# All 3x3 filters made within the first convolution, columns first, and half as many pixels transposed by TensorE ahead of the Gram matrix

## The chip, the cores and the metric

The kernel runs on one core of a Trainium2 chip. The metric is the device time of one execution in microseconds (us). The engines are TensorE (PE in the profile), VectorE (DVE), ScalarE (ACT), GpSimd (POOL) and SyncE (SP). Each works through its own queue in order. DMAs are issued from the queues of SP, POOL and ScalarE.

## The reference

Two bottleneck blocks of a residual network, one after the other, on an input of 64 images with 1024 channels and 14x14 pixels, in float32. One block, shortened:

```python
out = relu(bn(conv1x1(x,   w1) + b1))      # 1024 -> 256 channels
out = relu(bn(conv3x3(out, w2) + b2))      # 256 -> 256, padding 1
out =      bn(conv1x1(out, w3) + b3)       # 256 -> 1024
x   = relu(x + softplus(residual_scale)[0] * out)
```

`bn` takes mean and variance of each channel over all images and pixels (12544 values), so each convolution has to be finished, or its statistics known, before the next can begin.

## The kernel before

All 12544 pixels of the 256 inner channels stay on the chip in `y_all`, 128 channels in two halves. Products of 1x1 convolutions are made by a Strassen-Winograd scheme with seven products instead of eight: class `Seven` names them p1 to p7, and `stream` gives their order over the items, in which p4 and p3 of an item (`last`) come after p1 of the next one:

```python
for now in items:
    yield from now.p1()
    if before is not None:
        yield from before.last()
    yield from now.p6()
    ...
    yield from now.p2(); now.p5(); now.p7()      # each with yield from
```

The stages, in order:

1. **First convolution, layer 0** (about 6 to 322 us). Two images per load of x. The first two loads go through `plain_conv1`, the other thirty in fifteen items of `Conv1` with two loads each. p1, p6, p7 and p4 add up in one bank of the tag `ay` (two buffers); after p1, p6 and p7 ScalarE copies the bank out (`saved`, through `act`, which keeps program order). p2 goes to `ax`, p5 and p3 to `ap` (one buffer each), which VectorE empties with the sum of L346. VectorE also makes four sums of x per item (L354, L355, L356, L373) and the statistics (L349). Beside it, VectorE makes the transformed filters of the 3x3 convolution: `filters`, for six of the eight pieces (layer, input half, output half). The generator is advanced between items: 42 yields over 11 items. It lives in the last 3136 pixels of both halves of `y_all`, which are not yet written. A piece is loaded by SP (L178) into one buffer, its sums are L189, its factors L186, and its six results go to DRAM by POOL (L227).
2. **Second convolution, layer 0** (to about 611 us): a Winograd scheme `conv2`, which reads the filters `us` back from DRAM.
3. **`gram`, layer 0**: the Gram matrix of the normalized pixels, from which the statistics of the third convolution follow without computing it. ScalarE normalizes `y` in pieces of 256, 512, 800 and then seven times 1568 pixels, two halves each (`norm`, L504); `less` takes a centre off: on ScalarE for 1568 pixels in layer 0 (L1199), else on VectorE (L1201). The product needs pixels on the partitions, so they are transposed, 256 at a time (a "pair" of blocks):
   - `by_tensor`: four transposes on TensorE (L904) into PSUM, then a copy by VectorE (L910). The first `FIRST` = 12 pairs and the last one.
   - `by_vector`: SP and POOL first spread 1536 pixels over the partitions by 16 DMAs (`spread`, L896: ten on SP, six on POOL) into one of two `homes`, and VectorE then transposes six pairs out of it (L916). There are `STEPS` = 6 such spreads; spread k + 2 is issued when step k has been transposed.
   Six buffers `zt` lie between VectorE and TensorE. TensorE then multiplies each block by itself (`cp`, `ap`). In layer 0, `gram` also makes the last two pieces of the filters (1, 1, 0) and (1, 1, 1) on VectorE, in twelve portions, in three spare tiles of x.
4. **`conv3_stats`, `residual`**: the statistics of the third convolution, the scale and shift (`affine`), and the first image pair. Two of its eight products are made ahead (`made`), before the statistics; VectorE adds a product to x (L992).
5. **`fused`**, layer 0's third convolution beside layer 1's first one (to about 1315 us), then `conv2`, `gram` (about 1618 to 1695 us), `conv3_stats`, `residual` and `final` for layer 1.

PSUM banks are taken from `Psum`, which hands out tags by a cycle (in layer 1 `cy`, `cx`, two buffers each) unless a tag is named. A scheduler orders the instructions of an engine where they are not pinned by `keep_in_program_order`; TensorE's and `act`'s are pinned.

Of the kernel before, what the change touches and what calls it, by code (L numbers as in the profile page):

```python
# [38 lines left out]
AF = mybir.ActivationFunctionType  # L39
ALU = mybir.AluOpType  # L40

P = 128
# [3 lines left out]
CS = C // P  # L46
MS = M // P
G = 2
T = N // G
# [4 lines left out]
CH = 2  # L54
NZT = 6

FIRST, LAST = 12, 1
RUN = 3 * P
STEP = 4 * RUN
STEPS = (NPX - (FIRST + LAST) * CH * P) // STEP  # L60
# [6 lines left out]
GPX = GI * HW  # L67
RT, NF = 4, 6
# [5 lines left out]
FOUR = 0, 2, 3, 4, 5  # L74
NKS = [4 if i in FOUR else 5 for i in range(NF)]
NK = max(NKS)
D1D2, D0, D3, D1, D2 = range(5)
SUM, DIFF, D0M2, D3M1 = range(4)
ODD, EVEN = range(2)
# [10 lines left out]
def bottlenecks(ctx: ExitStack, tc: tile.TileContext, x, w1s, w2s, w3s, pars, out):  # L90
    nc = tc.nc
# [74 lines left out]

        tc.keep_in_program_order(nc.tensor.matmul(*args, **kw))  # L167

    def filters(eng, b, s, o, spare, pinned=False):

        first, second = spare
        w, n = 3 * P, NK * P
        g = first[:, : 3 * w].rearrange("p (r m) -> p r m", r=3)
        even, quad = first[:, 3 * w : 4 * w], first[:, 4 * w : 5 * w]
        rest, twice = first[:, 5 * w + n :], second[:, 4 * n : 4 * n + w]
        nc.sync.dma_start(out=g, in_=w2s[b][:, s, o])  # L178
        yield

        def run(ins):
            if pinned:
                tc.keep_in_program_order(ins)

        def scaled(to, v, by):
            run(eng.tensor_scalar(to, v, by, None, ALU.mult))  # L186

        def combined(*args):
            run(eng.tensor_tensor(*args))  # L189

        combined(even, g[:, 0], g[:, 2], ALU.add)
        scaled(quad, g[:, 2], 4.0)
        combined(quad, quad, g[:, 0], ALU.add)
        scaled(twice, g[:, 1], 2.0)
        parts = {
            0: (g[:, 0], None, None, 1.0 / 4),
            1: (even, g[:, 1], ALU.add, -1.0 / 6),
            2: (even, g[:, 1], ALU.subtract, -1.0 / 6),
            3: (quad, twice, ALU.add, 1.0 / 24),
            4: (quad, twice, ALU.subtract, 1.0 / 24),  # L200
            5: (g[:, 2], None, None, 1.0),
        }
        for i, (row, more, op, by) in parts.items():

            u = second[:, (i - 1) * n :] if more is not None else first[:, 3 * w :][:, (2 * w if i == 0 else 0) :]
            u = u[:, : NKS[i] * P].rearrange("p (k m) -> p k m", k=NKS[i])
            if more is not None:
                v = rest[:, :w]
                combined(v, row, more, op)
                row = v  # L210
            if i in FOUR:
                r0, r1, r2 = (row[:, k * P : (k + 1) * P] for k in range(3))
                ends = rest[:, w : w + P]
                combined(ends, r0, r2, ALU.add)
                combined(u[:, SUM], ends, r1, ALU.add)
                combined(u[:, DIFF], ends, r1, ALU.subtract)
                scaled(u[:, SUM : DIFF + 1], u[:, SUM : DIFF + 1], 0.5 * by)
                scaled(u[:, D0M2], r0, -by)
                scaled(u[:, D3M1], r2, by)
            else:  # L220
                row = row.rearrange("p (k m) -> p k m", k=3)
                scaled(u[:, D0 : D3 + 1], row[:, 0::2], by)
                scaled(u[:, D1D2], row[:, 1], by)
                combined(
                    u[:, D1 : D2 + 1], u[:, D0 : D3 + 1], u[:, D1D2 : D1D2 + 1].to_broadcast([P, 2, P]), ALU.subtract
                )
            nc.gpsimd.dma_start(out=us[b][i][:, s, o], in_=u)  # L227
            yield

    class Seven:  # L230
# [42 lines left out]
            yield from self.p3()  # L273
            yield from self.p4()

    def stream(items):

        before = None
        for now in items:
            yield from now.p1()  # L280
            if before is not None:
                yield from before.last()
            yield from now.p6()
            if before is not None:
                before.end()
            yield from now.p2()
            yield from now.p5()
            yield from now.p7()
            before = now
        yield from before.last()  # L290
        before.end()

    def act(*args, **kw):

        tc.keep_in_program_order(nc.scalar.activation(*args, **kw))  # L295
# [565 lines left out]
            finished.send(item)  # L861
            queue = queue[1:] + list(itertools.islice(made, 1))

    def conv3(psum, t, o, w3):
        ps = psum.tile()
        for s in range(MS):
            matmul(
                ps.rearrange("p (h l) -> p h l", h=H), w3[:, s, o, :], two(t, s), start=(s == 0), stop=(s == MS - 1)
            )
        return ps  # L870
# [75 lines left out]
                beside[k]()  # L946
        return g0, g1

    def conv3_stats(psum, one, grams, w3, mv):

        g0p, g1p = grams
        g0 = one.tile([P, M + 1], FP, tag="g0", name="g0")
# [188 lines left out]
    with tc.tile_pool(name="first", bufs=1) as one, tc.tile_pool(  # L1141
        name="first_x", bufs=4
    ) as xpool, ExitStack() as scope:
        psum = Psum(scope, ["ps"], ps=4, ay=2)
        w1 = load_w1(one, 0, nc.scalar)
        pair = [load_x(xpool, 0, t, 4 if t == 0 else 2) for t in range(2)]
        for b in range(2):
            p = keep.tile([P, NPAR], FP, tag=f"par{b}", name=f"par{b}")
            nc.scalar.dma_start(out=p, in_=pars[b][:, :NPAR])
            par.append(p)  # L1150
        masks.make_identity(nc, ident)
        w1 = combine_w1(w1, sums_tile(one, 1)[:, 0])

        for t, xt in enumerate(pair):
            plain_conv1(psum, t, xt, w1[0], par[0], stats1)


        spare = [y_all[:, i, NPX - CS * PX :] for i in range(MS)]
        pieces = [(0, 0, 0), (0, 0, 1), (0, 1, 0), (0, 1, 1), (1, 0, 0), (1, 0, 1)]
        work = itertools.chain.from_iterable(filters(nc.vector, *piece, spare) for piece in pieces)  # L1160
        total, free = (1 + NF) * len(pieces), T // 2 - 1 - CS // MS

        def items():
            for i, t in enumerate(range(2, T, 2)):
                xs = [load_x(xpool, 0, t + i) for i in range(2)]
                yield Conv1(psum, one, xs, (t, t + 1), w1, par[0], stats1)
                if i < free:
                    for _ in itertools.islice(work, total * (i + 1) // free - total * i // free):
                        pass

        for _ in stream(items()):
            pass

    for b in range(2):
# [9 lines left out]
        with tc.tile_pool(name=f"last_{b}", bufs=1) as one, tc.tile_pool(  # L1184
# [6 lines left out]
            with ExitStack() as scope:  # L1191
# [3 lines left out]
                    psum = Psum(scope, ["cy", "cx"], cy=2, cx=2, cp=2)  # L1195
                with tc.tile_pool(name=f"gram_{b}", bufs=1) as pool:
                    def less(k, y):
                        if b == 0 and y.shape[-1] == GPX:
                            nc.scalar.activation(y, y, AF.Identity, bias=minus_c[:, k : k + 1])  # L1199
                        else:  # L1200
                            nc.vector.tensor_scalar(y, y, minus_c[:, k : k + 1], None, ALU.add)  # L1201

                    def x_tile(name):
                        return xpool.tile([P, CS * PX], FP, tag="x", name=name)
# [75 lines left out]
```

## Time and profile before

| | |
|---|---|
| median of 3 runs | 2021.53 us (2021.08 to 2023.18) |
| profiled execution: time, span | 2024.42 us, 2022.6 us |
| TensorE matmul (PE) busy | 1955.8 us (97%) |
| VectorE busy | 1603.2 us (79%) |
| ScalarE busy | 927.8 us (46%) |
| GpSimd busy | 599.5 us (30%) |

The profile is that of one execution. A timeline line has start and duration in us, the engine, the line of the kernel, the operation, output<-inputs with their shapes, and how many instructions were merged; the bracket is the time for which the engine stood idle before, and what released it. A line of the list of waits has who waited for whom, us in total, how often, and the longest. A line of the table of windows has the stretch, then the busy us (and instructions) of PE, its weight loads, DVE, ACT and POOL, the clock granted to TensorE, the share of time for which the DMA engines were busy, and GB/s.

### The profile page before, as it was taken

What the parts mean: (1) busy time and instruction counts of PE and PEld (TensorE: products, weight loads), DVE (VectorE), ACT (ScalarE), POOL (GpSimd) and SP (SyncE); (2) the same over time, 40 slices, a digit from 0 to 9 for tenths busy, and PEclk for the clock granted to TensorE, in tenths of its full rate; (3) what the DMA queues carried; (4) which work ended last, traced back from release to release, by engine and by line L of the source; (5) the groups of instructions that cost most, each with busy time, mean ns of one, the idle gap of its engine ahead of it and who ended that gap; (6) DMA issues with size and microseconds to landing.
All of it is one profiled execution on the core that took longest, in us unless ns stands there. A gap on an engine that the chain in (4) does not pass through costs nothing.

```text
span 2022.6 us, 27698 instructions
## 1 busy us (share of the span) xinstructions
PE 1955.8 (97%) x9608; PEld 1647.0 (81%) x9608; DVE 1603.2 (79%) x3070; ACT 927.8 (46%) x1865; POOL 599.5 (30%) x648
## 2 busy tenths in 40 slices
PE   8989999999997999999999999989999899999998
PEld 4545557999996879999999999989999887555554
DVE  6878667999987667677777767689999874899997
ACT  1110113456568135555555555434666450555555
POOL 0101001121212223433343333311212130667665
PEclk9999999999998999999999999999999999999999
DMA  7756443656555814444444444255556455699998
GB/s 278 273 200 243 165 147 121 197 174 201 183 167 167 278 65 187 164 175 177 171 180 163 188 160 184 104 171 183 192 183 193 138 143 207 239 328 334 339 336 302
DMA packets 173661, 404.51 MB, mean 200 GB/s; under 512 B 11601, under 2 KB 141265, under 8 KB 157009
## 3 DMA queue, kind: packets, MB, share of 16 engines
q1 hardware_dynamic: 160608, 328.47, 47.5%
q10 hardware_dynamic: 5328, 50.86, 6.1%
q0 software_dynamic: 7584, 23.40, 3.5%
q8 instruction: 76, 1.25, 0.2%
q14 instruction: 65, 0.52, 0.1%
HBM read 267.95 MB, written 115.87 MB: 190 GB/s over the span
## 4 chain that ended last, share of the span: by engine, by line
PE 51%; DVE 8%; DMA 4%; SPq 1%; issue 1%; ACT 1%; POOL 0%; DVEq 0%; ACTq 0%; POOLq 0%
PE cy L167 13%; PE ay L167 9%; PE cp L167 8%; PE ap L167 5%; PE cx L167 4%; DMA x<-mid 3%; PE even L167 3%; PE odd L167 3%; PE ax L167 3%; PE m L167 2%; PE l L167 2%; DVE x L421 1%; DMA out<-x 1%; SPq L896 1%; DVE x L479 1%
## 5 line engine op out<-in xcount | busy, mean ns | idle before, releaser
L295 ACT ACTIVATE cu<-cy,scale 128x196 f32<-128x196 f32 (+1 forms) x552 | 256.9, 474 | 296.0 <-PE cy L167 288.1
L560 POOL TENSOR_TENSOR diffs<-r 128x448 f32<-128x448 f32 (+1 forms) x80 | 111.9, 1410 | 566.4 <-DVE r L598 290.8
L295 ACT ACTIVATE x<-x,shift 128x392 f32<-128x392 f32 x368 | 211.8, 614 | 68.8 <-POOL x L447 52.6
L421 DVE SCALAR_TENSOR_TENSOR x<-cp,scale,x 128x196 f32<-128x196 f32 (+1 forms) x368 | 177.9, 483 | 82.4 <-PE cp L167 81.3
L167 PE MATMUL cy<-ct,ws 128*128 128x196 f32 (+1 forms) x736 | 221.8, 383 | 2.5 <-ACT cu L295 2.5
L442 POOL TENSOR_TENSOR x<-x,cu 128x196 f32<-128x196 f32 (+1 forms) x184 | 167.9, 912 | 170.6 <-ACT cu L295 170.5
L167 PE MATMUL ay<-at,ws 128*128 128x196 f32 (+1 forms) x752 | 209.3, 381 | 1.0 <-ACT au L295 1.0
L447 POOL TENSOR_TENSOR x<-x,cu 128x392 f32<-128x392 f32 x124 | 125.9, 1015 | 190.7 <-DVE x L421 190.6
L295 ACT ACTIVATE au<-ay 128x196 f32<-128x196 f32 (+1 forms) x141 | 53.7, 381 | 250.3 <-PE ay L167 205.6
L167 PEld LDWEIGHTS ay<-at,ws 128*128 128x128 f32 x752 | 136.6, 190 | 35.4 <-ACT au L295 1.9
L167 PEld LDWEIGHTS cy<-ct,ws 128*128 128x128 f32 x736 | 133.6, 190 | 36.9 <-ACT cu L295 3.8
L468 POOL TENSOR_TENSOR x<-x,cu 128x392 f32<-128x392 f32 x120 | 125.1, 1042 | 82.1 <-DVE x L421 76.9
L167 PE MATMUL m<-sums,ua 128*128 128x224 f32 (+1 forms) x752 | 145.5, 336 | 0.0
L167 PEld LDWEIGHTS m<-sums,ua 128*128 128x128 f32 x752 | 131.4, 189 | 0.2
L167 PE MATMUL cp<-zt 128*128 128x257 f32 x392 | 121.4, 391 | 10.4 <-DVE zt L916 10.4
L421 DVE SCALAR_TENSOR_TENSOR x<-cx,scale,x 128x196 f32<-128x196 f32 (+1 forms) x184 | 89.1, 484 | 50.1 <-PE cx L167 49.8
L167 PE MATMUL cy<-y,w 128*128 128x196 f32 (+1 forms) x412 | 128.0, 397 | 0.0
L167 PE MATMUL cx<-y,w 128*128 128x196 f32 (+1 forms) x404 | 125.6, 396 | 0.7 <-DVE x L992 0.7
L167 PE MATMUL even<-v,ub 128*128 128x224 f32 (+1 forms) x640 | 123.8, 335 | 0.8 <-ACT even L654 0.8
L167 PE MATMUL odd<-v,ub 128*128 128x224 f32 (+1 forms) x640 | 123.8, 335 | 0.2
L167 PE MATMUL l<-diffs,ub 128*128 128x224 f32 (+1 forms) x640 | 122.0, 333 | 0.0
L167 PE MATMUL ap<-x,ws 128*128 128x196 f32 (+1 forms) x376 | 107.5, 390 | 10.2 <-DVE y L346 10.2
(214 smaller groups left out, 4360.1 us busy)
## 6 DMA issues: line engine op xcount, KB each, us to landing
x<-in_x SPq DMA_DIRECT2D x62, 1568.0 KB, 6.8
ub<-u SPq DMA_DIRECT2D x80, 768.0 KB, 4.8
x<-mid SPq DMA_DIRECT2D x32, 1568.0 KB, 10.0
mid<-x ACTq DMA_DIRECT2D x31, 1568.0 KB, 5.2
out<-x SPq DMA_DIRECT2D x124, 392.0 KB, 6.8
ua<-u SPq DMA_DIRECT2D x96, 256.0 KB, 3.1
ub<-u SPq DMA_DIRECT2D x16, 1024.0 KB, 6.3
home<-y SPq DMA_DIRECT2D x90, 96.0 KB, 3.8
```

Of the source, the lines that this page charges most:

```text
L167: tc.keep_in_program_order(nc.tensor.matmul(*args, **kw))
L295: tc.keep_in_program_order(nc.scalar.activation(*args, **kw))
L421: nc.vector.scalar_tensor_tensor(v, bank, self.scale[:, o : o + 1], v, ALU.mult, ALU.add)
L442: nc.gpsimd.tensor_add(self.part(1, 1), self.part(1, 1), u3)
L447: nc.gpsimd.tensor_add(v, v, self.u12)
L468: nc.gpsimd.tensor_add(v, v, self.u12[:, i * self.n : (i + 1) * self.n])
L479: nc.vector.tensor_scalar(v, v, self.shift[:, o : o + 1], 0.0, ALU.add, ALU.max)
L560: nc.gpsimd.tensor_sub(diffs, r[:, :, :, :WH], r[:, :, :, WH:])
L896: queue.dma_start(out=x[32 * i : 32 * i + 32, :, j], in_=y_all[32 * j : 32 * j + 32, :, a : a + RUN])
```

## The change

`filters` becomes one generator for all eight pieces. It adds up the columns first, for all three rows together, and then the rows; sums and scalar_tensor_tensor run on VectorE, factors on ScalarE through `act`; a piece is loaded while the one before is worked on, into the other of two buffers. It has eleven steps per piece. `stream` calls `beside` six times per item, which advances the generator by one or two steps, so that all eight pieces are made within the first convolution. The filters leave `gram`, with their spare tiles. `FIRST` goes from 12 to 6, so `STEPS` from 6 to 7. `less` runs on VectorE throughout. The banks of `made` and of `conv3_stats` are named instead of taken from the cycle.

```diff
-FIRST, LAST = 12, 1
+FIRST, LAST = 6, 1
...
+FSTEPS = 11
...
-    def filters(eng, b, s, o, spare, pinned=False):
+    def filters(pieces, spare):
         first, second = spare
...
+        n, w = 4 * P, 3 * P
+        def view(v, a, k):
+            return v[:, a * P : (a + k) * P].rearrange("p (k m) -> p k m", m=P)
+        rows = first[:, : 3 * n].rearrange("p (r k m) -> p r k m", r=3, m=P)
+        c2, c4, c3 = (view(first, 12 + 4 * i, 4) for i in range(3))
+        c1 = view(second, 18, 5)
+        loads = []
+        def load(piece):
+            b, s, o = piece
+            g = second[:, len(loads) % 2 * 3 * w :][:, : 3 * w]
+            nc.sync.dma_start(out=g.rearrange("p (r m) -> p r m", r=3), in_=w2s[b][:, s, o])
+            loads.append(g.rearrange("p (r k m) -> p r k m", r=3, m=P))
         def run(ins):
-            if pinned:
-                tc.keep_in_program_order(ins)
+            tc.keep_in_program_order(ins)
...
+        def sums(to, a, b, op):
+            run(nc.vector.tensor_tensor(to, a, b, op))
+        def sums_with(to, a, by, b):
+            run(nc.vector.scalar_tensor_tensor(to, a, by, b, ALU.mult, ALU.add))
+        load(pieces[0])
+        for piece, following in itertools.zip_longest(pieces, pieces[1:]):
+            b, s, o = piece
+            g = loads[-1]
+            def scaled(v, by):
+                act(v, v, AF.Copy, scale=by)
+            def out(i, u, a=0):
+                nc.gpsimd.dma_start(out=us[b][i][:, s, o, a : a + u.shape[1]], in_=u)
+            act(rows[:, :, D0M2], g[:, :, 0], AF.Copy, scale=-2.0)
+            act(rows[:, :, D3M1], g[:, :, 2], AF.Copy, scale=2.0)
+            sums(rows[:, :, SUM], g[:, :, 0], g[:, :, 2], ALU.add)
+            yield
+            sums(rows[:, :, DIFF], rows[:, :, SUM], g[:, :, 1], ALU.subtract)
+            yield
+            sums(rows[:, :, SUM], rows[:, :, SUM], g[:, :, 1], ALU.add)
+            if following is not None:
+                load(following)
+            yield
+            r0, r1, r2 = (rows[:, i] for i in range(3))
+            sums(c2, r0, r2, ALU.add)
+            yield
+            sums_with(c4, r2, 4.0, r0)
+            scaled(r0, 1.0 / 8)
+            out(0, r0)
+            yield
+            sums(c2, c2, r1, ALU.subtract)
+            scaled(r2, 1.0 / 2)
+            out(5, r2)
+            yield
+            sums_with(c3, r1, 2.0, c4)
+            scaled(c2, -1.0 / 12)
+            out(2, c2)
+            yield
+            sums_with(c4, r1, -2.0, c4)
+            scaled(c3, 1.0 / 48)
+            out(3, c3)
+            yield
+            sums(g[:, 0], g[:, 0], g[:, 2], ALU.add)
+            scaled(c4, 1.0 / 48)
+            out(4, c4)
+            yield
+            sums(c1[:, :3], g[:, 0], g[:, 1], ALU.add)
+            yield
+            sums(c1[:, 3:], c1[:, 0:3:2], c1[:, 1:2].to_broadcast([P, 2, P]), ALU.subtract)
+            scaled(c1, -1.0 / 6)
+            for to, a, e in ((D0, 0, 1), (D1D2, 1, 2), (D3, 2, 5)):
+                out(1, c1[:, a:e], to)
             yield
...
-    def stream(items):
+    def stream(items, beside=lambda: None):
             yield from now.p1()
             if before is not None:
+                beside()
                 yield from before.last()
+                beside()
             yield from now.p6()
             if before is not None:
                 before.end()
+            beside()
             yield from now.p2()
+            beside()
             yield from now.p5()
+            beside()
             yield from now.p7()
+            beside()
...
-    def conv3(psum, t, o, w3):
-        ps = psum.tile()
+    def conv3(psum, t, o, w3, tag=None):
+        ps = psum.tile(tag=tag)
...
-    def conv3_stats(psum, one, grams, w3, mv):
+    def conv3_stats(psum, one, grams, w3, mv, tags):
...
-            t0, t1 = psum.tile(half * P), psum.tile(half * P)
+            t0, t1 = (psum.tile(half * P, tag) for tag in tags[2 * h : 2 * h + 2])
...
-        pieces = [(0, 0, 0), (0, 0, 1), (0, 1, 0), (0, 1, 1), (1, 0, 0), (1, 0, 1)]
-        work = itertools.chain.from_iterable(filters(nc.vector, *piece, spare) for piece in pieces)
-        total, free = (1 + NF) * len(pieces), T // 2 - 1 - CS // MS
+        pieces = list(itertools.product(range(2), range(MS), range(MS)))
+        work = filters(pieces, spare)
+        total, calls, count = FSTEPS * len(pieces), 6 * (T // 2 - 1 - CS // MS), itertools.count(1)
+        def beside():
+            i = next(count)
+            for _ in itertools.islice(work, total * i // calls - total * (i - 1) // calls):
+                pass
...
-        for _ in stream(items()):
+        for _ in stream(items(), beside):
             pass
...
                     def less(k, y):
-                        if b == 0 and y.shape[-1] == GPX:
-                            nc.scalar.activation(y, y, AF.Identity, bias=minus_c[:, k : k + 1])
-                        else:
-                            nc.vector.tensor_scalar(y, y, minus_c[:, k : k + 1], None, ALU.add)
+                        nc.vector.tensor_scalar(y, y, minus_c[:, k : k + 1], None, ALU.add)
...
-                    if b == 0:
-                        second = x_tile("spare")
-                        work = [filters(nc.vector, 1, 1, o, (x_tile("spare"), second), pinned=True) for o in range(MS)]
-                        for piece in work:
-                            next(piece)
-                        work = itertools.chain.from_iterable(work)
-                        beside.update({1 + 3 * i: partial(next, work) for i in range(MS * NF)})
                     grams = gram(psum, pool, homes, aff, less, beside)
-                    made = [conv3(psum, 0, o, w3) for o in range(2)]
+                    made = [conv3(psum, 0, o, w3, "cx" if b else "ay") for o in range(2)]
...
-                    conv3_stats(psum, pool, grams, w3, mv3)
+                    conv3_stats(psum, pool, grams, w3, mv3, ("cy", "cp", "cy", "cp" if b else "cx"))
```

More of the change, by code (lines that the diff above doesn't have):

```diff
@@ L167, in matmul @@
         tc.keep_in_program_order(nc.tensor.matmul(*args, **kw))
-    def filters(eng, b, s, o, spare, pinned=False):
+    def filters(pieces, spare):
         first, second = spare
[L174 to L179, printed above, removed]
-        def run(ins):
-            if pinned:
-                tc.keep_in_program_order(ins)
[L185 to L219, printed above, removed]
-            else:
[L221 to L227, printed above, removed]
@@ L1158, in bottlenecks @@
         spare = [y_all[:, i, NPX - CS * PX :] for i in range(MS)]
-        pieces = [(0, 0, 0), (0, 0, 1), (0, 1, 0), (0, 1, 1), (1, 0, 0), (1, 0, 1)]
-        work = itertools.chain.from_iterable(filters(nc.vector, *piece, spare) for piece in pieces)
-        total, free = (1 + NF) * len(pieces), T // 2 - 1 - CS // MS
+        pieces = list(itertools.product(range(2), range(MS), range(MS)))
[5 more added lines that the diff above has]
+                pass
         def items():
-            for i, t in enumerate(range(2, T, 2)):
+            for t in range(2, T, 2):
                 xs = [load_x(xpool, 0, t + i) for i in range(2)]
                 yield Conv1(psum, one, xs, (t, t + 1), w1, par[0], stats1)
-                if i < free:
-                    for _ in itertools.islice(work, total * (i + 1) // free - total * i // free):
-                        pass
-        for _ in stream(items()):
+        for _ in stream(items(), beside):
             pass
@@ L1197, in less @@
                     def less(k, y):
-                        if b == 0 and y.shape[-1] == GPX:
-                            nc.scalar.activation(y, y, AF.Identity, bias=minus_c[:, k : k + 1])
-                        else:
-                            nc.vector.tensor_scalar(y, y, minus_c[:, k : k + 1], None, ALU.add)
+                        nc.vector.tensor_scalar(y, y, minus_c[:, k : k + 1], None, ALU.add)
                     def x_tile(name):
```

## The prediction

> **What bounds the kernel now.** I read the page first: TensorE is busy 97% of the span, so time is to be had only where TensorE idles or runs at a low clock. The list of TensorE's waits says for whom it idles; a table of windows says when; the timelines of single engines say why.
>
> TensorE's waits over the whole span (us in total, times, longest):
>
> ```profile
> PE cy L904 <- DVE y L1201: 13.9, 2, 7.0
> PE ap L167 <- DVE y L346: 10.8, 6, 4.9
> PE cp L167 <- DVE zt L916: 10.4, 8, 3.6
> ```
>
> The first are the waits for the norm before each `gram`, one per layer. The second is the first convolution (`Conv1`). The third is inside `gram`. The windows around the second (busy us of each engine and instructions, clock, DMA share, GB/s):
>
> ```profile
> 100.00:150.00 50.00, 43.40 (x123) 24.08 (x122) 35.94 (x79) 5.24 (x10) 4.39 (x8) 0.93 0.57 211
> 150.00:200.00 50.00, 46.13 (x138) 26.04 (x139) 46.24 (x112) 4.65 (x9) 6.48 (x12) 1.00 0.64 227
> 200.00:250.00 50.00, 50.00 (x154) 28.88 (x153) 31.64 (x32) 5.74 (x11) 0.00 (x0) 1.00 0.47 173
> ```
>
> TensorE is full once the filters are done (from 200), and not before. VectorE and TensorE in that stretch:
>
> ```profile
> 117.14 0.56 DVE L189 TENSOR_TENSOR y<-y 128x384 f32<-128x384 f32 x1 [6.95 <-DMA u<-y]
> 126.30 0.62 DVE L346 SCALAR_TENSOR_TENSOR y<-ap,par,au 128x392 f32<-128x392 f32 x1
> 126.97 5.53 PE L167 MATMUL ap<-x,ws 128*128 128x392 f32 x8 [4.91 <-DVE y L346]
> 132.34 2.80 PE L167 MATMUL ay<-at,ws 128*128 128x392 f32 x8
> ```
>
> A filter instruction waits 6.95 us for the store of the filter before it; behind it VectorE works through a backlog, the sum that empties bank `ap` (L346) comes late, and TensorE stands 4.91 us and then needs 5.53 us for eight matmuls instead of 2.80.
>
> The second `gram`, which has no filters beside it, is the pattern for both:
>
> ```profile
> 1617.47 26.60 ACT L504 ACTIVATE y<-y,shift,scale 128x256 f32<-128x256 f32 x20 [1.41 <-DVE shift L1106]
> 1643.68 1.29 DVE L916 STREAM_TRANSPOSE zt<-home 128x512 f32<-128x512 f32 x2
> 1644.44 0.70 PE L167 MATMUL cp<-zt 128*128 128x257 f32 x2 [0.93 <-DVE zt L916]
> 1661.19 0.70 PE L167 MATMUL cp<-zt 128*128 128x257 f32 x2 [0.72 <-DVE zt L916]
> ```
>
> ScalarE needs until 1644.07 for all norms; VectorE's first transpose of a spread piece (`by_vector`) comes at 1643.68, just as the twelve pairs transposed by TensorE run out.
>
> **The change part by part.** A profiled execution took 2024.42 us (span 2022.6); that is 2.9 above the median, 2021.53. I sum differences within the span and take them from the median.
>
> *Filters in the first convolution.* An undisturbed item of `Conv1` (seven products) takes 223.24 - 204.81 = 18.43 us. The eight items from 42.86 to 204.81 took 161.95, against 8 x 18.43 = 147.44: 14.5 us lost. Its own work is some 10.3 us of VectorE per item (four 128x1568 sums at 1.70 us from start to start, three L346 at 0.53, four statistics at 0.48). Filters cost it 45.1 + 25.7 = 70.8 us busy for six pieces (L189 and L186), 11.8 each, handed over in lumps of four yields. A piece now costs, from start to start: five 128x384 sums at 0.47, two 128x512 sums at 0.60, three 128x512 scalar_tensor_tensor at 0.60 (worked out from 0.42 at 336 and 0.77 at 672 elements), one 128x256 at 0.34: 5.7 us, 45 us for eight. `beside` deals out 88 steps over 66 calls, eight steps per full item, 4.1 us; VectorE then has 14.4 of 18.43 us, in lumps of one or two steps (under 1.3 us). The tightest need is the sum after p7, which p3 of the next round needs 5.3 us (two products) later: one 1.70 sum, at most 1.3 of filters and 0.53 fit. Buffers are written again six to ten steps (over 13 us) after their store is issued, and a store lands in 5.7 us, so the 6.95 us wait should go. Taken: all of it, **-14.5 us**; from below -8, if the lumps still catch one item in two.
>
> What this adds: per piece seven factors on ScalarE, in its queue ahead of the copies of `ay` that TensorE needs. The nearest row, 128x392 out of PSUM, took 0.497 us; a 128x512 should take about 0.6, so 4.8 us per piece, 3.5 per item, on an engine busy 5 of 50 us. The copy after p7 must be done 2.63 us later; a factor before it waits for a VectorE step dealt out after p5, which is done by then. Taken as nothing; from above 1.3 us per item (rival one). POOL's stores go from 6 to 8 a piece at 0.55 us: POOL does nothing else there. SP's eight filter loads stand between loads of x; they used to wait for the one buffer behind VectorE (36 us of SP's waits), now there are two buffers. Loads plus stores: 2.2 MB per piece, about 90 GB/s on top of 173, as in the first 100 us, where TensorE had no wait. Nothing.
>
> *`gram`, both layers.* Out of layer 0's: twelve filter stores on POOL and two loads on SP, 22.9 us of VectorE, and 14 centrings of 128x1568 from ScalarE, now on VectorE (1.03 us each), as layer 1 always had it. From its first transpose to the first plain matmul, layer 0 took 703.77 - 618.48 = 85.3 us, layer 1 1694.58 - 1618.60 = 76.0.
>
> Into both: FIRST 6 for 12, seven spreads for six (10 more DMAs on SP, 6 more on POOL each), six times four transposes less on TensorE (6 x 0.44 = 2.6 us). The built order of VectorE tells what replaces them: eleven of the fourteen big centrings stand ahead of the first spread transpose. The eleventh waits for ScalarE's eleventh big norm: 1644.07 - 3 x 1.58 = 1639.3, plus 1.03 = 1640.4, plus 0.67 for the transpose: 1641.1. (The first spread, issued from about 1627.4 and landing some 10.5 us later, is there before.) But TensorE's six pairs, steady from 1621.1 and 1.75 us each, are used up at about 1632.6 with their last product. TensorE then stands for 8.5 us, and starts cold.
>
> The price of a cold start is where a rule must be weighed. Rows: after 4.91 us of idleness eight matmuls took 2.73 us too long; after 3.58 us in layer 0's `gram` the first two pairs took 4.25 us for 2.62:
>
> ```profile
> 651.41 1.22 PE L167 MATMUL cp<-zt 128*128 128x257 f32 x2 [3.58 <-DVE zt L916]
> ```
>
> The Trainium skill (TensorE: Matmul & The Clock Gate, What's actually happening) has TensorE at half clock after an idle window of about 3.4 us and back after as long a busy one, so at most about 1.7 us lost per restart, with idleness up to 3.4 us possibly free. The first row, 2.73, is more than the rule allows. The rule speaks against halving FIRST; by it (1.7 per `gram`) the whole sum would be -8.0, by the dearer row -6.0, by the row of these same matmuls (1.6) -8.2. I take the last.
>
> Then 42 pairs by VectorE at 1.313 (55.1), one by TensorE (1.75), and a short wait for the third spread: the first piece is transposed by 1647.1, a spread took 10 to 12.2 us from there, so 1657.1 to 1659.3, when TensorE gets there at about 1658.5; taken 0.7. Sum: 1641.1 + 1.6 + 55.1 + 1.75 + 0.7 = 1700.3, so 81.7 for 76.0: **+5.7 us in layer 1** (3.4 with neither cold start nor third wait, 8.5 if each later spread takes the full 12.2), and 81.7 for 85.3, **-3.6 us in layer 0**.
>
> *Banks in `conv3_stats` and `residual`.* In layer 0 two statistics products move to other free banks; the next bank of `residual` is `cx`, free by then: nothing (TensorE's one wait was 0.16). In layer 1 both ready results now lie in `cx`, which has two buffers, and the cycle hands `residual`'s third product `cx` again. Before:
>
> ```profile
> 1709.64 2.96 PE L167 MATMUL cx<-y,w 128*128 128x392 f32 x4
> 1712.39 1.63 PE L167 MATMUL cy<-y,w 128*128 128x392 f32 x4
> 1714.76 1.56 PE L167 MATMUL cx<-y,w 128*128 128x392 f32 x4 [0.73 <-DVE x L992]
> ```
>
> The third and fourth products ran while VectorE worked out the scale; only the fifth waited for L992. Now the third waits for that same L992, and the fourth, whose `cy` is free, is queued behind it. Both move past 1714.7 at the low clock they had: 2.75 + 1.45 = **+4.2 us** (2.6 at full clock, 5 if colder). The final stage behind is full of matmuls (49.6 of 50 us), so it passes this on.
>
> *Loads of x.* Three spare tiles go, so x of layer 0 comes earlier; nothing waited for it (L992 waited for the scale). In layer 1 two of five come after the last spread, still 40 us before use. Nothing.
>
> Sum: -14.5 - 3.6 + 5.7 + 4.2 = -8.2. 2021.5 - 8.2 = 2013.3.
>
> **The rivals.** *Rival one, slower.* ScalarE becomes the gate: it keeps its order, so a factor waiting for a late VectorE step holds the copy after p7, and p4 waits. Losing 0.75 us in each of eleven items eats the whole 8.2. At 1.3 us per item the first convolution gains nothing, and the `gram`s and banks leave +6.3: 2027.8. For it: ScalarE's copies already waited 6.5 us for L186. Against: 2.63 us of slack, and an undisturbed VectorE. Chance 0.12. *Rival two, no change.* The lumps still catch some items (-8 to -10) and both `gram`s end at the long side (+8.5 and -0.8), so about 2020. Chance 0.13. *Rival three, much faster.* The seventh spread arrives for free, as the halving suggests: TensorE goes on at 1632.6 and each `gram` ends 11 us sooner than above, about 1992. The order of VectorE and ScalarE's pace speak against it. Chance 0.03. The forecast: 0.72.
>
> **How the numbers follow.** About 0.2% (4 us) is what a measurement can tell from no change. The forecast's own range, with -10 to -14.5 for the filters, 3.4 to 8.5 per `gram` against 5.7 and 2.6 to 5 for the banks, is 2008 to 2018, nearly all faster. To hold 8 in 10 it reaches into rival two: 2008 to 2020.5. Faster 0.75, same 0.13, slower 0.12.
>
> **What would show it.** In the profile after: no wait of `ap` for VectorE's sum before 320 us and 18.43 us per item, right; waits of `ay` for ScalarE there, rival one. In `gram`, one wait of `cp` for `zt` of about 8.5 us per layer with a slow first pair, and 81 to 82 us from first transpose to first plain matmul; under 73 would make rival three right. After layer 1's statistics, a wait of `cx` of about 5 us for the sum that is L992 before. If the filters give under 8 us, or a `gram` differs by over 3 us from 81.7, a step of mine is wrong.

## The result and the profile after

| | before | changed |
|---|---|---|
| median of 6 runs each, on one chip | 2022.86 us | 2015.66 us (2014.43 to 2019.02) |
| ratio to before | | 0.9964 (95% interval 0.9947 to 0.9981) |
| profiled execution: time, span | 2024.42, 2022.6 us | 2014.53, 2012.5 us |

The changed kernel is faster by 0.36%, 7.3 us with an interval of 4 to 11; the prediction had 8.2. (On the later chips the kernel before had medians of 2023 to 2025 us, so the experiments are compared by their ratios, or stage by stage.)

The table of windows of the changed kernel's first convolution, columns as in the one of before:

```profile
100.00:150.00 50.00, 50.00 (x153) 28.85 (x153) 40.94 (x54) 13.57 (x26) 8.62 (x16) 1.00 0.69 249
150.00:200.00 50.00, 50.00 (x154) 28.85 (x153) 43.25 (x55) 13.32 (x25) 7.54 (x14) 1.00 0.71 248
200.00:250.00 50.00, 50.00 (x154) 28.85 (x153) 38.29 (x47) 13.03 (x25) 8.59 (x16) 1.00 0.70 256
```

TensorE (second number) is now full in every one of them, at full clock (1.00); it was 43.40 and 46.13 in the first two. VectorE is at 38 to 43 of 50 us, ScalarE at 13.

The list of TensorE's waits, whole span (us in total, times, longest):

```profile
PE cp L169 <- DVE zt L948: 16.3, 2, 8.2
PE cy L936 <- DVE y L1233: 13.9, 2, 7.0
...
PE cx L169 <- DVE x L1025: 5.0, 1, 5.0
...
PE ap L169 <- DVE y L378: 0.3, 1, 0.3
```

The wait of `ap` for VectorE's sum, 10.8 us before, is gone (L378 is L346 of before). Eight short waits of `cp` for `zt` have become one of 8.2 us per `gram`, and a wait of `cx` for `residual`'s sum (L1025) is new.

Inside layer 1's `gram` VectorE and TensorE read, in their timelines:

```profile
1619.34 1.04 DVE L1233 TENSOR_SCALAR y<-y,minus_c 128x1568 f32<-128x1568 f32 x1 [0.55 <-ACT y L536]
1620.29 1.30 DVE L948 STREAM_TRANSPOSE zt<-home 128x512 f32<-128x512 f32 x2
```

```profile
1612.54 0.38 PE L169 MATMUL ap<-zt 128*128 128x129 f32 x2
1621.06 1.23 PE L169 MATMUL cp<-zt 128*128 128x257 f32 x2 [8.13 <-DVE zt L948]
1622.07 0.64 PE L169 MATMUL ap<-zt 128*128 128x129 f32 x2
1622.50 1.07 PE L169 MATMUL cp<-zt 128*128 128x257 f32 x2
1623.36 0.64 PE L169 MATMUL ap<-zt 128*128 128x129 f32 x2
1623.79 1.07 PE L169 MATMUL cp<-zt 128*128 128x257 f32 x2
1624.64 0.44 PE L169 MATMUL ap<-zt 128*128 128x129 f32 x2
```

The six pairs from TensorE are used up at 1612.9. The eleventh big centring, which waited for ScalarE's norm, ends at 1620.4; the transposes follow, and TensorE comes back cold: three blocks take 1.44, 1.29 and 1.13 us from start to start instead of 0.66, so 1.9 us are lost after 8.13 us of idleness. Both this and the 2.73 us of the first convolution before exceed the 1.7 us that the prediction had estimated as the most per restart from the Trainium skill (TensorE: Matmul & The Clock Gate, What's actually happening). The granted clock tells why they differ. In both traces it stood at 0.50 for 6.8 us, and what is lost is half of the part that comes after the restart: about 3.7 us here (1621.06 to 1624.7), 5.3 us there (126.97 to 132.3).

After layer 1's statistics (TensorE's timeline):

```profile
1691.16 1.93 PE L169 MATMUL ax<-ones,q 128*128 128x1 f32 x16
1698.06 2.95 PE L169 MATMUL cx<-y,w 128*128 128x392 f32 x4 [4.98 <-DVE x L1025]
1700.81 2.70 PE L169 MATMUL cy<-y,w 128*128 128x392 f32 x4
1703.34 1.48 PE L169 MATMUL cx<-y,w 128*128 128x392 f32 x4
```

The third product waits for the sum, and it and the fourth, behind it, run at the low clock.

Stage by stage, from starts in TensorE's timeline (us). "First convolution" runs from the first matmul of `Conv1` to the first of layer 0's `conv2`; `gram` from its first transpose to its first plain product; "banks" from there to the first product of layer 1's last stage (`final`), whose bank is `cy`:

| | first conv. | `gram` 0 | `gram` 1 | banks |
|---|---|---|---|---|
| before | 293.72 | 85.29 | 75.98 | 27.53 |
| changed | 279.25 | 81.38 | 81.28 | 30.74 |
| difference | -14.5 | -3.9 | +5.3 | +3.2 |

These four come to -9.9 of the -10.1 us by which the spans differ. The rest nearly cancels: -2.8 between the two `gram`s, +0.9 in layer 0's `conv2`, +1.6 in `final`.

### The profile page after: what moved, and what is told of

It reads as the page before. It is cut to its first block, busy times and chain, and to the rows that moved or that the text cites. A ratio compares the mean times of both kernels' runs of the same rounds, so it can differ in the third digit from the quotient of the medians.

```text
span 2012.5 us, 27547 instructions
## 1 busy us (share of the span) xinstructions
PE 1947.0 (97%) x9560; PEld 1640.9 (82%) x9560; DVE 1586.7 (79%) x2844; ACT 941.2 (47%) x1915; POOL 617.1 (31%) x676
## 3 DMA queue, kind: packets, MB, share of 16 engines
q8 instruction: 75, 1.23, 0.2%
## 4 chain that ended last, share of the span: by engine, by line
PE 80%; DVE 12%; DMA 5%; ACT 1%; issue 1%; POOL 1%; SPq 0%; DVEq 0%; ACTq 0%; POOLq 0%
PE ay L169 16%; PE cy L169 13%; PE cp L169 11%; PE ap L169 10%; PE even L169 6%; PE odd L169 6%; PE m L169 5%; PE ax L169 5%; PE l L169 4%; PE cx L169 4%; DMA x<-mid 3%; DVE x L453 2%; PE ps L169 1%; DMA out<-x 1%; DVE sums L589 1%
## 5 line engine op out<-in xcount | busy, mean ns | idle before, releaser
L169 PE MATMUL cx<-y,w 128*128 128x196 f32 (+1 forms) x412 | 129.7, 402 | 5.0 <-DVE x L1025 5.0
L169 PE MATMUL cp<-y,ws 128*128 128x196 f32 (+1 forms) x368 | 113.8, 391 | 3.3 <-DVE x L453 1.8
```

## The experiments

**The two later parts undone.** FIRST back at 12:

```diff
-FIRST, LAST = 6, 1
+FIRST, LAST = 12, 1
```

> The changed kernel with FIRST back at 12 (six spreads), all else as changed. Mine: halving FIRST is a loss of its own. Each gram, from its first transpose to its first plain matmul, goes from 81.3 us back to about 76, the 8.2 us wait of cp for zt falls into waits of under 3 us, and the time is about 10.5 us below the changed kernel (ratio to the kernel before about 0.991). Rival a, the halving saves what it takes off TensorE (24 transposes per layer, 2.6 us): 5 us above the changed kernel, grams of 84. Rival b, the length of gram is set by something else in the change (centring on VectorE, the pace of the spreads): no difference, grams stay at 81.

Measured: ratio to before 0.9903 (0.9890 to 0.9917), `gram`s of 75.03 and 76.39 us. In layer 1's `gram` TensorE's longest wait for `zt` is this one:

```profile
1621.04 0.60 PE L169 MATMUL cp<-zt 128*128 128x257 f32 x2
1621.47 0.38 PE L169 MATMUL ap<-zt 128*128 128x129 f32 x2
1622.79 0.70 PE L169 MATMUL cp<-zt 128*128 128x257 f32 x2 [0.93 <-DVE zt L948]
```

The twelfth pair ends as the first spread piece is transposed, and the clock stays up (the first two matmuls take 0.70 us, not 1.23). The two `gram`s are 11.2 us shorter, and by the ratios this kernel is 0.6%, some 12 us, below the changed one. Both rivals fall: the 24 transposes are cheaper than the gap that they filled.

Layer 1's banks from the cycle:

```diff
-made = [conv3(psum, 0, o, w3, "cx" if b else "ay") for o in range(2)]
+made = [conv3(psum, 0, o, w3, None if b else "ay") for o in range(2)]
...
-conv3_stats(psum, pool, grams, w3, mv3, ("cy", "cp", "cy", "cp" if b else "cx"))
+conv3_stats(psum, pool, grams, w3, mv3, (None,) * 4 if b else ("cy", "cp", "cy", "cx"))
```

> The changed kernel with the PSUM banks of layer 1's two ready products and its statistics taken from the cycle again (cx and cy) instead of named. Mine: the third product of residual no longer waits 5.0 us for the sum with x; from the first ready product to the last product of the first image 24.2 us instead of 27.4, and about 3 us less in all. Rival: the last stage cannot start its own work earlier (its sums on VectorE come behind the scale), so it waits as much longer there and the time is the same.

Measured: 0.9942 (0.9929 to 0.9955), 28.25 us for 30.74. The wait of `cx` for L1025 is gone, but the small products ahead of it happened to run at a lower clock here (the sixteen `ones` products took 3.55 us for 1.93) and hid a part. By the ratios some 4 us are gained, with intervals that overlap (the changed kernel's begins at 0.9947, this one's ends at 0.9955); what settles the size is this stage in all fourteen kernels: median 27.5 us (25.7 to 28.3) in the seven with banks from the cycle, 30.8 (30.7 to 32.3) in the seven with named ones. The rival, that the last stage takes it back, is not supported: from its first product to the last matmul it takes 297.3 us here and 297.2 in the changed kernel.

Both together, and then with layer 0's banks from the cycle too (the `tag` arguments left out throughout):

> FIRST at 12 and layer 1's banks from the cycle, the filters as changed. Mine: the two gains add up, about 14 us below the changed kernel, near 2001 us, ratio to the kernel before about 0.989: what is left of the change is the filters. Rival: they overlap (the end of gram and the waits behind it hide one another), and it is no better than FIRST at 12 alone.

> As the kernel with FIRST at 12 and layer 1's banks from the cycle, with layer 0's banks from the cycle too, so that only the filters and the place of the centring differ from the kernel before. It asks for the 2.8 us by which the changed kernel was quicker between layer 0's gram and layer 1's, which I had not predicted. Mine: the named banks of layer 0 let the products between the statistics and residual follow more densely, so this is 1.5 to 2 us slower than with them. Rival: it was a different clock in that execution, or conv2 of layer 1, and the two are equal.

Measured: 0.9887 (0.9871 to 0.9904), median 2000.99 us; and 0.9872 (0.9858 to 0.9885), median 1999.88 us. The gains add up, and the second, whose interval overlaps the first's, has the lowest median of this study, 25 us below before, with what is left of the change: the filters in the first convolution, and the centring on VectorE. My idea that layer 0's named banks are worth 2 us falls: from layer 0's first ready product to the first of `fused` took 24.96 us in the changed kernel, but 29.03 with FIRST at 12 and the same banks, 26.24 in the first of this pair and 25.31 in the second. So the -2.8 us between the `gram`s is scatter between executions as far as these runs can tell. That kernel's lines after the statistics:

```profile
1679.89 1.93 PE L169 MATMUL ax<-ones,q 128*128 128x1 f32 x16
1681.67 2.86 PE L169 MATMUL cx<-y,w 128*128 128x392 f32 x4
1684.33 1.92 PE L169 MATMUL cy<-y,w 128*128 128x392 f32 x4
1686.79 1.55 PE L169 MATMUL cx<-y,w 128*128 128x392 f32 x4 [0.54 <-DVE x L1025]
```

Two products run while the scale is worked out; the wait moves to the fifth and shrinks from 4.98 to 0.54 us.

**What freed the first convolution?** Factors on VectorE instead of ScalarE:

```diff
-act(v, v, AF.Copy, scale=by)
+run(nc.vector.tensor_scalar(v, v, by, None, ALU.mult))
```

(and the two factors of a piece's first step likewise.)

> The changed kernel with the seven factors of each filter piece on VectorE, in their places among the sums, instead of on ScalarE. It asks whether the move to ScalarE was needed, or whether fewer sums and longer-lived buffers were enough. A factor on 128x512 should take about 0.5 us on VectorE (as the centring of that shape), so 3.7 us a piece, 2.7 an item, and VectorE has 17.1 of 18.43 us to do. Mine: still just room on average, but less slack than one 1.70 us sum, so some items lose: 281 to 286 us from Conv1's first matmul to the second convolution, against 279.25. Rival a: ScalarE carried nothing of the gain, 279.25 stays. Rival b: VectorE is then the bound and the loss is back as before: 290 or more.

Measured: 0.9961 (0.9945 to 0.9977); first convolution 279.24 us. The table of windows of this kernel:

```profile
100.00:150.00 50.00, 50.00 (x153) 28.85 (x153) 45.59 (x70) 5.74 (x11) 8.74 (x15) 1.00 0.70 250
150.00:200.00 50.00, 50.00 (x154) 28.85 (x153) 47.55 (x70) 5.75 (x11) 8.60 (x15) 1.00 0.68 247
```

VectorE is busy for up to 47.55 of 50 us and TensorE loses nothing: rival a, and my 281 to 286 was wrong. ScalarE carried none of the gain, and how much of VectorE's time is free on average is not what counts either. (A 128x512 factor took 0.42 us there, 0.62 on ScalarE.)

The steps handed over eight at once, between two items (six calls of `beside` after the `yield` of an item, none in `stream`):

```diff
 yield Conv1(psum, one, xs, (t, t + 1), w1, par[0], stats1)
+for _ in range(6):
+    beside()
...
-for _ in stream(items(), beside):
+for _ in stream(items()):
```

> The changed kernel with its filter steps handed over as before: eight at once between two items, not one or two at six places of an item. It tells whether the dealing out is what freed the first convolution. Mine: no. The scheduler spreads the steps in VectorE's built order in either case (two to four filter sums between two sums of x), so from the first matmul of Conv1 to the second convolution it takes 279 to 282 us (279.25 as changed, 293.72 before). Rival: the lumps made the loss, and at least half of the 14.5 us comes back: 286 or more.

Measured: 1.0335 (1.0263 to 1.0407); first convolution 348.13 us. I was wrong by 66 us. The rival's range holds the number, but the loss is almost five times that of the kernel before, and the lumps alone do not make it, as the next run shows. One of the eleven waits of this kind, on ScalarE and then on TensorE:

```profile
76.65 1.56 ACT L327 ACTIVATE y<-y 128x640 f32<-128x640 f32 x3 [6.61 <-DVE y L196]
80.50 0.63 ACT L327 ACTIVATE y<-y 128x512 f32<-128x512 f32 x1 [2.29 <-DVE y L199]
81.04 0.48 ACT L327 ACTIVATE au<-ay 128x392 f32<-128x392 f32 x1
```

```profile
74.09 2.80 PE L169 MATMUL ap<-x,ws 128*128 128x392 f32 x8
81.57 2.88 PE L169 MATMUL ay<-at,ws 128*128 128x392 f32 x4 [4.68 <-ACT au L327]
```

TensorE had finished p1, the product that ScalarE is to copy, by about 71.6. The copy starts at 81.04: the lump's factors stand ahead of it in ScalarE's pinned order, waiting for VectorE sums that the scheduler had spread over the item; p6, which adds to the same bank, waits for the copy. This is rival one of the prediction, at the copy after p1 instead of the one after p7, and it is dear: eleven waits of 2.4 to 5.1 us, 45 us in all, and after nine of them a stretch at clock 0.50. In the changed kernel ScalarE waits almost as long for filter sums (77 us in all, 85 with the lumps), but `ay` waits for ScalarE only 1.2 us, at the first and the last item, as before: dealt out, the factors stand between the copies and not all ahead of one.

The same lumps, with the factors on VectorE:

> The new filters in lumps of eight steps between two items, with their factors on VectorE. With factors on ScalarE these lumps took 348.1 us from Conv1's first matmul to the second convolution, with TensorE waiting 45 us for ScalarE's copies; dealt out, either engine gives 279.25. Mine: the lumps cost through ScalarE's queue alone (factors that wait for VectorE stand ahead of the copies that TensorE needs), so without factors there it is 279 to 285 us. Rival: the lumps themselves cost, on whichever engine: 300 or more.

Measured: 0.9955 (0.9943 to 0.9968); first convolution 282.92 us. Without factors on ScalarE the lumps cost 3.7 us, not 69, so my expectation held.

One buffer for the loaded piece:

```diff
-g = second[:, len(loads) % 2 * 3 * w :][:, : 3 * w]
+g = second[:, : 3 * w]
...
 sums(c1[:, :3], g[:, 0], g[:, 1], ALU.add)
+if following is not None:
+    load(following)
 yield
```

(and the load at the third step taken out)

> The changed kernel with one buffer for a loaded filter piece instead of two: the next piece is loaded only when the last but one step of this one has read the buffer, so VectorE and ScalarE come to its first step before it has landed (7.6 us from issue to landing, and one or two places at which steps are dealt out, 3 us each, in between). Nothing else is added. Mine: such a wait is what stalled TensorE before; VectorE waits 2 to 5 us for the load, seven times, the factors queued on ScalarE hold copies of ay up as well, and 4 to 10 us of the 14.5 come back (283 to 289 us). Rival: it is the amount of VectorE's work alone that matters, the waits are taken up by slack, and 279.25 stays.

Measured: 1.0008 (0.9990 to 1.0026); first convolution 286.35 us, 7.1 longer. The waits of ScalarE and of TensorE in that stretch:

```profile
ACT y L327 <- DMA y<-in_w: 24.9, 5, 8.6
```

```profile
PE ay L169 <- ACT au L327: 5.6, 2, 5.0
```

So a wait for a DMA at the head of a shared queue does cost what I had supposed, here through ScalarE: five waits of ScalarE, one of which holds TensorE for 5.0 us. Two buffers are needed with the factors there; with the factors on VectorE this was not tried.

**The old filters, dealt out and pinned.** Four combinations of two edits to the kernel before: `beside` in `stream` with the old generator, and its instructions pinned:

```diff
-filters(nc.vector, *piece, spare) for piece in pieces
+filters(nc.vector, *piece, spare, True) for piece in pieces
```

> The kernel before with one edit: its old filter instructions (six pieces, sums and factors on VectorE, one set of buffers) are dealt out at six places of an item and pinned in that order. Mine: the waits of VectorE for the store of the filter before stay, and so does nearly all of the loss: 290 to 294 us from Conv1's first matmul to the second convolution (293.72 before, 279.25 as changed). Rival: fine dealing alone frees TensorE: 283 or less.

> The kernel before with one edit: its filter instructions are pinned in program order, still handed over four yields at once between two items. With the run that also dealt them out (280.54 us from Conv1's first matmul to the second convolution, 293.72 before) it parts two things: dealing and pinning. In the built order of before, VectorE has up to 26 filter instructions in a row, hoisted ahead of the sums; pinned, they stand behind those that were written earlier. Mine: the hoisting makes the bunches, a bunch comes to the next store before it has landed, and pinning alone brings most of it: 280 to 285 us, with waits of VectorE for stores of under 5 us in all (14.1 before). Rival: dealing out is what counts, 288 or more.

> The kernel before with its old filter instructions handed over at six places of an item, but not pinned, so that the scheduler may hoist them as before. The fourth of the four combinations. Mine (hoisting is the cause): 288 to 294 us from Conv1's first matmul to the second convolution, with waits of VectorE for stores of 8 to 15 us. Rival (dealing is the cause): 284 or less.

Measured:

| old filters, six pieces | ratio to before | first conv. | VectorE's filter sums (L189) wait for stores | its sums out of PSUM (L346) wait for stores |
|---|---|---|---|---|
| as before | 1 | 293.72 | 14.1 us in 3 | none |
| dealt out | 0.9990 (0.9977 to 1.0003) | 290.45 | 12.5 in 2 | none |
| pinned | 0.9957 (0.9941 to 0.9973) | 282.60 | 2.5 in 1 | 4.6 in 1 |
| dealt out and pinned | 0.9952 (0.9920 to 0.9985) | 280.54 | 3.0 in 2 | 6.5 in 1 |

The first expectation failed: the old filters, with all their instructions on VectorE, cost next to nothing once they are dealt out and pinned. The other two hold, except that pinned VectorE's waits for stores come to 7.1 us in all and not to under 5. VectorE's list of waits in the first convolution, dealt out but unpinned:

```profile
DVE y L189 <- DMA u<-y: 12.5, 2, 7.0
```

and VectorE's and TensorE's, pinned alone:

```profile
DVE y L346 <- DMA u<-y: 4.6, 1, 4.6
PE ap L167 <- DVE y L346: 3.1, 1, 3.1
```

Pinning does most of it. Unpinned, the scheduler puts the filters in bunches, up to 18 instructions with nothing else between them (not 26, as I had written); five bunches have 16 or more, dealt out or not, since it sorts them again. Pinned, one such bunch is left; dealt out and pinned, none over 14. I read it so: a bunch overtakes the stores that its buffers wait for, and then stands at the head of VectorE's queue. In the trace of before, TensorE's waits of 4.9 and 2.5 us each follow one of VectorE's two longest waits for a store (6.95 and 5.22 us). Dealing out leaves these two; it takes away three short ones, 3.0 us together, and that is its 3.3 us.

Two things qualify this. Pinning also spreads the work: the last filter instruction comes at 242.9 us instead of 197.0. That VectorE was merely too full before is unlikely, since with the factors of the new filters on it VectorE was fuller (45.59 and 47.55 of 50 us, against 35.94 and 46.24) and TensorE lost nothing; but no run parts the bunches from this. And so late, the last stores are still under way when the sums of L346 come to the pixels that the filters had been lent: this wait of 4.6 us is behind the 3.1 us that TensorE still loses with pinning alone, while dealt out as well a wait of 6.5 us costs it nothing.

**Why is TensorE left waiting in `gram`?** Centrings pinned among the transposes, those of a later piece only before the step that needs them:

```diff
 x = ready.pop(0)
+centred(1)
 for i in range(RUN // (CH * 32)):
```

(`centred(n)` issues the next n pieces' centrings, pinned; five pieces before the first spread.)

> The changed kernel (FIRST at 6) with the centrings of gram pinned among the transposes: six of the fourteen big ones stand ahead of VectorE's first transpose of a spread piece instead of eleven. It asks what holds TensorE for 8.2 us behind the sixth pair: the centrings, as I predicted, or the landing of the first spread, which is issued at 1607.6 us of the changed kernel's trace with ten issues of 0.79 us on SyncE and so should be there at about 1618 to 1619, while the transposes start at 1620.3. Mine: both are close together, the spread is next in line; the wait falls by 1 to 2.5 us only, and the grams take 79 to 80.3 us instead of 81.3, about 2 to 4 us in all. Rival a (centrings alone): the wait falls under 4 us and the grams to 76 or 77. Rival b: the spread was late anyway, 81.3 stays.

Measured: 0.9955 (0.9938 to 0.9971); `gram`s of 82.27 and 80.31 us. VectorE in layer 1:

```profile
1609.93 1.98 DVE L1242 TENSOR_SCALAR y<-y,minus_c 128x1568 f32<-128x1568 f32 x2
1617.02 3.68 DVE L956 STREAM_TRANSPOSE zt<-home 128x512 f32<-128x512 f32 x6 [5.11 <-DMA home<-y]
```

The centrings are done at 1611.9, and VectorE then stands 5.11 us for the spread, 10.7 us after its first issue at 1606.36. TensorE's wait falls only from 8.13 to 6.07 us, and of these 2.1 us the `gram` keeps 1.0: the stretch at clock 0.50 reaches further past the restart (5.8 us, against 3.7). In layer 0 the spread took 13.4 us (612.68 to 626.05), and that `gram` gained nothing, as rival b had it. Mine holds at the edge in layer 1 and fails in layer 0. Rival a falls: behind the centrings stands the spread.

## Why the prediction was right, and where its reasons were not

- *Filters in the first convolution, -14.5.* Exact in size: 279.25 us for 293.72, every item of the changed kernel 18.43 us; each of the seven kernels with the new filters dealt out and two buffers took 279.24 or 279.25. That all of the loss would go was right for reasons that were half wrong, so the size was in part luck. I put the loss down to too much work on VectorE and to the wait for the store, and the gain to fewer, shorter instructions and factors on ScalarE. The runs show the work was affordable as it was: pinned and dealt out, the old instructions lose 1.3 us (six pieces), and the new ones lose nothing with their factors on either engine. What freed TensorE was the order, pinned above all, which the diff brings by dropping `if pinned` and which the prediction does not mention. That the new filters need it too is carried over from the old ones: the new ones were not run unpinned. I had the wait for the store in the profile (6.95 us) but did not ask why a store was still under way, which the built order of VectorE would have told.
- *ScalarE at nothing, bounded by 1.3 us per item.* Right as built. As a bound it was too narrow: the waits for VectorE that I named reached 5.0 us in an item as soon as the factors came in lumps.
- *Halving FIRST, +5.7 in layer 1 and -3.6 in layer 0.* Measured +5.3 and -3.9. The first product after the gap comes 22.46 us after the first transpose, predicted 22.5; the wait was 8.13 for 8.5, the cold start 1.9 for 1.6. The third spread (taken as 0.7) did not hold TensorE. All that layer 0 gained came from what left it: with FIRST at 12 it takes 75.0 to 76.3 us, so halving cost it 5 to 6 us as well. That this was the filters is likely, as before they stood between VectorE's transposes there, but ScalarE's centrings left at the same time, and no run parts the two. The first spread, which I had landing 2.5 us ahead of the last of the eleven centrings, lands about 2 us ahead of it in layer 1 (19.7 us after the first transpose with the centrings out of its way, against 21.8 for their end), so taking the centrings away brings little.
- *Banks, +4.2.* Measured +3.2, and +3.3 between the medians of the two sets of seven. The mechanism is as predicted; that the size is near is luck, for two terms were off in opposite directions. The sum came 2.0 us sooner after the first ready product than I had carried over from before, mostly because the small products ran at full clock (1.93 us for 3.55), and the fourth product took 2.53 us at the low clock instead of 1.45. In the three kernels with named banks whose small products took 3.55 us, this stage takes 32.3 us, 4.8 more than before.
- *Nothing for the rest.* -2.8, +0.9 and +1.6 us in stages whose code is the same or nearly; between executions these stages differ by as much. The -2.8 I could tie to no edit.
- *The range.* Rival two's own terms, a gain of 8 to 10 against +8.5 - 0.8 + 4.2, come to 2023 to 2025 and not to about 2020, and the long ends of the forecast's own terms reach beyond its 2018 in the same way, to about 2024. The measured time lies well inside, so nothing hung on it.
- *Rival three* (the spread comes for free) is out; rival one is real, but has to be provoked.

## What to carry to other kernels

Before work is made cheaper or moved to another engine, look at the built order of the queue that it shares: here one argument that pins background work in order brought 11 of the 14.5 us, with no instruction made cheaper. On a shared in-order queue what matters is what the head of the queue waits for; deal background work out near the work that it stands between, above all where one engine's factor waits for another's sum. And judge each part of a bundle by itself: two of the three here took back some 14 of the 24 us that the first (with what it lifted out of `gram`) had brought.

## What the runs showed that I had not expected

- TensorE stayed at 50.00 of 50 us beside a VectorE busy for 47.55, but lost 69 us in this stage when ScalarE, busy for 57 of 300 us, had its queue in the wrong order.
- Sixteen DMAs of 96 KB that spread a piece took 10.7 us in layer 1 and 13.4 in layer 0 from the first issue to the first transpose, though over all spreads a transfer lands 3.4 us (median) after its own issue. The ten issues on SyncE alone stretch over 6.2 and 6.5 us from the first to the last, and the last of them took 4.2 us to land in layer 1 and 6.3 in layer 0.
- With the same code, the sixteen one-column products after the statistics took 1.93 to 3.55 us, depending on the execution, and with them goes the granted clock: 1.93 at 0.98 to 1.00, 3.55 at 0.50. In the kernel before the clock fell to 0.50 at 1705.9, while TensorE stood for nothing: it had been at one-column products since 1702.55.
- A wait shorter than those of the prediction can bring the low clock too. With the old filters dealt out but unpinned, the clock fell to 0.50 for 3.4 us after a wait of 2.82 us, and the eight matmuls behind it took 4.59 us for 2.80, as the line below shows. In two other runs it stayed up after 3.04 and 3.09 us.

```profile
150.64 4.59 PE L167 MATMUL ap<-x,ws 128*128 128x392 f32 x8 [2.82 <-DVE y L352]
```
